# Matrices of shared places by two VectorE comparisons in place of a comparison, a matmul and a copy, with every phase's steps set anew

## The chip, the cores and the metric

The kernel runs on one core of a Trainium2 chip. Its time is the device time of one execution in microseconds; lower is better. Five queues matter: TensorE (PE, whose weight loads the profile shows apart as PEld), VectorE (DVE), ScalarE (ACT), GpSimd (POOL) and the DMA-issuing queue SP. Each engine executes its own instructions in the order in which they stand in the program.

## The reference

32 graphs of 512 nodes with 128 features each go through two layers of a residual graph network with a layernorm after each. The adjacency matrix is sparse, about one entry in sixteen.

```python
adj = adj + eye;  d = adj.sum(2) ** -0.5
x = layernorm(x + (d[:, :, None] * adj * d[:, None, :]) @ (x @ weight) + bias)

m_j = x @ W1[:D];  m_i = x @ W1[D:]
msg = gelu(layernorm(m_j[:, None] + m_i[:, :, None] + b1))     # one vector for each edge
agg = einsum('bijo,bij->bio', msg, adj)
x = layernorm(x + layernorm(concat([x, agg]) @ W2 + b2))
```

The costly part is `msg`: a 128-wide vector, its layernorm and its gelu for every edge.

## The kernel before, in words

**Edges.** A graph's nodes are cut into C = 4 chunks of 128 (P). The kernel works on edges in blocks of 128 by 128 (16 blocks in a graph, numbered n), lists each node's neighbours by half block with max-8 instructions on DVE, and treats the first four of each list (`SLOTS`) as four slots, t = 0 to 3. Edges that did not fit there share two further slots, t = 4 and 5 (`SHARED = 2`): all remaining edges of a block get a running place from 1 to 256, and a place is served by one of 128 rows in one of the two shared slots.

**Units.** A unit (t, q) is one slot of one chunk. A graph has 20 units in this order: (0,0) to (2,3), then (3,0), (3,1), (4,0), (3,2), (4,1), (3,3), (5,0), (5,1). They are numbered 0 to 19 here, so units 14, 16, 18 and 19 are of shared slots. For each unit PE gathers and adds the two nodes' parts into a tile `u` in PSUM, two tiles in turn (`pairs`, L855 to L875); for t < 4 DVE adds the rest and moves it to SBUF (`sums`, L881); ACT applies the gelu, eight instructions for a unit (`messages`, L914); POOL makes the weighted gather matrices (`weights`, L897 and L901); and PE adds up the result (`aggregate`, L928 and L938). The order is written out by hand in one loop over g, the running number of the unit: at an even g the pairs of two units, at an odd g the aggregates of two earlier ones, messages and sums between them.

**Phases.** Everything else that a graph needs is cut into steps (Python generators, one step up to each `yield`): `layer0` (first layer, transposes, the keys), `lists`, `factors`, `more`, `counts`, `spots`, `sending`, `picks`, `parts`, `own_edges`, `finish`. A unit has two half units, so a graph has 40. The table `PLAN` gives for each step of each phase the half unit, relative to the start of the graph's first unit, at which the step's instructions are put into all queues, between the messages of that half unit. Steps with negative numbers run while the graph before is worked on; modulo 40 they show what they share a half unit with. Within one half unit the phases stand in a fixed order: finish, layer0, lists, factors, more, counts, spots, sending, picks, parts, own_edges.

**Around the change.** `counts` numbers the shared edges: `over` and its sums on DVE give a count for each node and block, a matmul with a triangle matrix (`po`, L620) the running sums, and DVE makes `first` and `last` from it (L623, L625): node p of block n owns the places `first < e <= last`. `spots` turns this into `sj`, one row of zeros and ones over 256 places for each node and block. It works on a pair of blocks at a time: `up_to` marks places up to `last` (L647, two DVE instructions); since `first` of a node is `last` of the node before it, a matmul with `step_down` (ones on the diagonal, minus ones beside it) takes the difference of neighbouring rows (`pj`, L660); a DVE copy moves it from PSUM to `sj` (L655). `sending` multiplies the blocks with `sj` (L676: two matmuls for each of 16 blocks) and ACT copies each result to `sent` (L672). `picks` reads `sent` and writes index lists to DRAM, from which the units of t = 4 and 5 gather.

**PSUM.** One pool `ps` of three banks serves in turn, in program order, all phases: the transposes of `layer0`, its `psup` (read by ACT in L334 and L339), its `pconv` (read by DVE in `y`, L364), `po`, `pj` and the `pl` of `sending`. A bank is used again when its reader has finished.

**Patterns.** The constant `places` is kept as 3 by 86 elements with a gap after each 86.

Of the kernel before, what the change touches and what calls it, by code (L numbers as in the profile page):

```python
# [9 lines left out]
BF16 = mybir.dt.bfloat16  # L10
# [3 lines left out]
ALU = mybir.AluOpType  # L14
# [4 lines left out]
P = 128  # L19
# [6 lines left out]
SHARED = 2  # L26
# [3 lines left out]
DEV = 12  # L30

PLAN = {
    "layer0": [-44, -41, -39, -39, -38, -36, -36, -34, -31, -31, -31, -31, -30, -30, -29, -25, -25, -25, -24, -23, -20, -18, -17, -13],
    "lists": [-20, -20, -20, -20, -18, -18, -18, -18, -17, -13, -13, -13, -13, -13, -13, -13, -12, -11, -10, -9, -8],
    "parts": [-18, -13, -13, -9, -9, -9, -8, -7, -7],
    "factors": [-11, -11, -10, -8, -7, -7, -7, -7, -6],
    "more": [-20, -18, -11, -10, -9, -9, -8, -8, -8, -6, -6, -6, -6, -6, -6, -6, -6, -6],
    "counts": [-5, -5, -4, -4, -4],
    "own_edges": [-6, -4, 21, 29],
    "spots": [-3, -2, -2, -1, 0, 2, 3, 4, 5, 8],  # L40
    "sending": [9, 9, 9, 9, 9, 9, 9, 9, 9, 9, 9, 9, 9, 9, 9, 9, 9],
    "picks": [13, 15, 16, 17, 18, 20, 22, 23, 23, 23, 23, 23],
    "finish": [43, 48, 49, 50, 55, 57, 59, 61, 62, 70, 74, 75, 77],
}


# [19 lines left out]
def sparse_path(ctx, tc, x, adj, w0, b0, w1, b1, g1, be1, w2, b2, g2, be2, out, most, flag):  # L66
# [21 lines left out]
    nc = tc.nc  # L88
# [3 lines left out]
    const = ctx.enter_context(tc.tile_pool(name="const", bufs=1))  # L92
# [13 lines left out]
    ident_h = const.tile([P, P], BF16, name="ident_h")  # L106
# [7 lines left out]
        out=stri, in_=stri, compare_op=ALU.is_ge, fill=0.0, base=-1, pattern=[[1, P]], channel_multiplier=-1  # L114
# [8 lines left out]
    place_w = node.tile([P, 3, n_places // 3], F32, tag="t1", name="place_w")  # L123
    nc.gpsimd.iota(
        place_w,
        pattern=[[n_places // 3, 3], [1, n_places // 3]],
        base=1,
        channel_multiplier=0,
# [1 line left out]
    )  # L130
    places = const.tile([P, 3, n_places // 3 + 2], BF16, name="places")[:, :, : n_places // 3]
    nc.vector.tensor_copy(places, place_w)
    step_down = const.tile([P, P], BF16, name="step_down")
    nc.gpsimd.memset(step_down, -1.0)
    nc.gpsimd.affine_select(
        out=step_down, in_=step_down, compare_op=ALU.is_equal, fill=0.0, base=-1, pattern=[[1, P]],
        channel_multiplier=-1,
    )
    nc.vector.tensor_add(step_down, step_down, ident_h)
    place_k = const.tile([P, SHARED], F32, name="place_k")  # L140
    nc.gpsimd.iota(
        place_k, pattern=[[P, SHARED]], base=1, channel_multiplier=1, allow_small_or_imprecise_dtypes=True
# [6 lines left out]
        nth, pattern=[[1, KEPT]], base=0, channel_multiplier=0, allow_small_or_imprecise_dtypes=True  # L149
# [40 lines left out]
    parts = node.tile([P, 3, D], F32, tag="f0", name="be_parts")  # L190
# [8 lines left out]
    for k in range(4):  # L199
# [5 lines left out]
        out=chunk_of, in_=chunk_of, compare_op=ALU.not_equal, fill=1.0, base=0, pattern=[[-1, C], [-C, P // C]],  # L205
        channel_multiplier=1,
# [50 lines left out]
    def bank(key):  # L257
        return ps.tile([P, 512], F32, tag="ps", name=key)
# [376 lines left out]
    def spots(b):  # L635

        st = state[b]
        sj = big.tile([P, C * C, SHARED * P], F32, tag="sj", name=f"sj_{b}")
        st["sj"] = sj
        last = st["last"]  # L640
        n_pairs = C * C // 2
        up_to, pt = {}, {}
        for k in range(n_pairs + 2):
            if k < n_pairs:
                up_to[k] = node.tile([P, 2, n_places], BF16, tag="up_to", name=f"up_to_{b}_{k}", bufs=2)
                for n in range(2):
                    nc.vector.tensor_scalar(  # L647
                        up_to[k][:, n, :].rearrange("p (k e) -> p k e", k=3),
                        places,
                        last[:, 2 * k + n : 2 * k + n + 1],  # L650
                        None,
                        ALU.is_le,
                    )
            if k >= 2:
                nc.vector.tensor_copy(  # L655
                    sj[:, 2 * k - 4 : 2 * k - 2, :], pt.pop(k - 2).rearrange("p (n e) -> p n e", n=2)
                )
            if 1 <= k <= n_pairs:
                pt[k - 1] = bank(f"pj_{b}_{k}")
                nc.tensor.matmul(pt[k - 1], step_down, up_to.pop(k - 1)[:, :, : SHARED * P], start=True, stop=True)  # L660
            yield

    def sending(b):
# [127 lines left out]
    last, more_t = SLOTS - 1, (SLOTS, SLOTS + 1)  # L791
# [171 lines left out]
    for rank, phase in enumerate((finish, layer0, lists, factors, more, counts, spots, sending, picks, parts, own_edges)):  # L963
        for n, at in enumerate(PLAN[phase.__name__]):
            for b in range(B):
                steps_at.setdefault(at + b * n_steps_b, []).append((rank, b, n, phase))
# [288 lines left out]
def kernel(  # L1255
# [33 lines left out]
    with ExitStack() as inner:  # L1289
        sparse_path(inner, tc, *args, most, flag)  # L1290
# [36 lines left out]
```

## Time and profile before

| what | value |
|---|---|
| median of three runs | 3031.48 us (3030.92 to 3032.12) |
| the profiled execution's own time | 3032.46 us |
| its span, first to last instruction | 3030.8 us |
| granted TensorE clock, mean | 0.988 |
| PE, busy share of the span | 94% |
| PEld | 79% |
| DVE | 80% |
| ACT | 84% |
| POOL | 68% |

The profiled execution lies 1.0 us above the median, so its span and the median can be taken for the same number within 0.03%. Matmuls are pipelined and their ends are modelled, so that a busy PE need not be a PE at its rate; the distance from the start of one matmul to that of the next says more. The busy times of neighbouring DVE instructions can overlap in the same way.

### The profile page before, as it was taken

The page shows a single profiled execution, that of the slowest core. Times are in us where ns is not written, and L with a number is a line of the kernel's source. Part 1 is how long each engine was busy: PE and PEld are TensorE (multiplying, and loading weights), DVE is VectorE, ACT ScalarE, POOL GpSimd, SP SyncE. Part 2 cuts the span into 40 slices and gives each one's busy share as a digit, 9 for nine tenths or more (in the row PEclk, how much of TensorE's full clock was granted, in tenths as well). Part 3 has the DMA queues.
Part 4 walks back from the last instruction along what each step waited for, and adds up shares of the span by engine and source line. Part 5 has one row for each costly group of instructions (what it writes and reads, how often), then busy time and mean ns, then how long its engine had stood idle before and what let it go on. Part 6 is the DMA issues. An engine that isn't in the chain of part 4 may idle for free. (4 is left out here: it accounts for less than half of the span.)

```text
span 3030.8 us, 96573 instructions
## 1 busy us (share of the span) xinstructions
PE 2844.0 (94%) x35522; PEld 2379.5 (79%) x35713; DVE 2423.9 (80%) x9803; ACT 2560.8 (84%) x7873; POOL 2065.0 (68%) x2525
## 2 busy tenths in 40 slices
PE   4999999999999999999999999999999999999996
PEld 2788878878778788788788788788787887887875
DVE  6777888777988777988778988778887779887782
ACT  2888888888888888888888888888888888888885
POOL 3576766676776677766667766767666767766765
PEclk7999999999999999999999999999999999999998
DMA  2344443444443444443445433444434444434441
GB/s 58 73 94 99 103 96 78 94 98 99 98 98 77 97 91 106 98 91 82 90 93 112 96 82 81 98 99 101 96 78 96 97 100 98 98 77 97 88 92 45
DMA packets 593025, 276.14 MB, mean 91 GB/s; under 512 B 456112, under 2 KB 576048, under 8 KB 592544
## 3 DMA queue, kind: packets, MB, share of 16 engines
q1 hardware_dynamic: 592320, 269.41, 40.5%
q8 instruction: 284, 4.65, 0.6%
q14 instruction: 197, 1.61, 0.2%
q0 software_dynamic: 224, 0.46, 0.1%
HBM read 155.45 MB, written 13.63 MB: 56 GB/s over the span
## 5 line engine op out<-in xcount | busy, mean ns | idle before, releaser
L914 ACT ACTIVATE m<-m,r 128x128 f32<-128x128 f32 x4096 | 1263.7, 392 | 18.6 <-DVE m L881 18.5
L881 DVE TENSOR_TENSOR m<-u,ac 128x1024 f32<-128x1024 f32 x512 | 609.6, 1211 | 329.8 <-PE u L863 319.2
L897 POOL TENSOR_TENSOR sw<-mt,a_t 128x512 f32<-128x512 bf16 x512 | 616.4, 1224 | 18.0 <-DMA mt<-s 15.1
L928 PE MATMUL agg<-m,sw 128*64 128x128 f32 x8192 | 515.3, 277 | 3.1 <-POOL sw L897 2.8
L928 PEld LDWEIGHTS agg<-m,sw 128*64 128x64 f32 x8192 | 444.6, 137 | 69.9 <-issue 34.2
L855 PEld LDWEIGHTS <-s 64*128 64x128 bf16 x12288 | 364.8, 94 | 140.0 <-issue 98.2
L870 PE MATMUL u<-ac,sj 128*128 128x128 f32 x2048 | 441.4, 297 | 24.4 <-DVE m L881 18.4
L855 PE MATMUL u<-c,s 64*128 64x128 bf16 x12288 | 433.4, 218 | 13.3 <-DVE s L818 13.1
L243 POOL TENSOR_SCALAR ve_l<-mv_l 128x4 f32<-128x4 f32 x96 | 33.7, 351 | 468.3 <-DVE mv_l L240 468.3
L870 PEld LDWEIGHTS u<-ac,sj 128*128 128x128 f32 x2048 | 325.1, 192 | 32.6 <-DVE m L881 25.7
L872 PE MATMUL u<-c,s 128*128 128x128 bf16 x3072 | 339.5, 220 | 0.0
L672 ACT COPY sent<-pl 128x328 f32<-128x328 f32 x512 | 221.2, 432 | 112.8 <-PE pl L676 57.2
L901 POOL TENSOR_TENSOR sw<-mt,sent 128x512 f32<-128x512 bf16 x256 | 291.4, 1163 | 12.2 <-PE agg L938 8.5
L676 PE MATMUL pl<-a_t,sj 128*128 128x164 f32 x2048 | 297.8, 304 | 0.8 <-ACT aggt L766 0.8
L676 PEld LDWEIGHTS pl<-a_t,sj 128*128 128x128 f32 x2048 | 286.4, 190 | 7.7 <-ACT sent L672 6.6
L914 ACT ACTIVATE m<-u,r_s 128x128 f32<-128x128 f32 x1024 | 272.2, 379 | 8.0 <-PE u L875 5.9
L938 PEld LDWEIGHTS agg<-m,sw 128*128 128x128 f32 x2048 | 236.4, 192 | 52.8 <-issue 51.6
L872 PEld LDWEIGHTS <-s 128*128 128x128 bf16 x3072 | 259.9, 99 | 12.1
L938 PE MATMUL agg<-m,sw 128*128 128x128 f32 x2048 | 250.6, 278 | 0.1
L513 DVE FIND_INDEX8 idx<-top,key 128x8 uint32<-128x64 f32 x1024 | 210.1, 218 | 0.0
L581 DVE MATCH_REPLACE8 key<-top,key 128x64 f32<-128x64 f32 x1024 | 205.8, 208 | 0.0
L863 PE MATMUL u<-be_d,sd_rows 64*128 64x512 bf16 x1024 | 195.5, 378 | 0.0
(214 smaller groups left out, 5641.8 us busy)
## 6 DMA issues: line engine op xcount, KB each, us to landing
raw<-idx_d SPq DMA_DIRECT2D x256, 256.5 KB
raw<-idx_ds SPq DMA_DIRECT2D x64, 513.0 KB
a_nat<-in_adj_dram SPq DMA_DIRECT2D x32, 1024.0 KB
sd_rows<-sd_d SPq DMA_DIRECT2D x768, 12.0 KB
xs<-in_x_dram SPq DMA_DIRECT2D x32, 256.0 KB
out_dram<-o_sb SPq DMA_DIRECT2D x32, 256.0 KB
sd_d<-sd_p SPq DMA_DIRECT2D x256, 12.0 KB
mt<-s SPq DMA_TRANSPOSE x192
```

Source lines behind the costliest of these rows:

```text
L513: nc.vector.max_index(idx[:, n - 1, h, :], top[:, n - 1, h, :], half(n - 1, h))
L672: nc.scalar.copy(sent[:, n - 1], pt[:, : SHARED * WIDE].rearrange("p (k w) -> p k w", w=WIDE))
L676: nc.tensor.matmul(pt[:, k * WIDE : (k + 1) * WIDE], sj[:, n, k * P : (k + 1) * P], at[:, n, :], start=True, stop=True,)
L855: nc.tensor.matmul(pu[:, h, c, :], s[halved(h), c, q * P : (q + 1) * P], c3[halved(h), k, c, :], start=(c == 0 and k == 0), stop=False,)
L870: nc.tensor.matmul(pu[:, h, c, :], place, st["ac"][:, q_h, 0, :], start=(c == 0), stop=False)
L872: nc.tensor.matmul(pu[:, h, c, :], s[:, c, q_h * P : (q_h + 1) * P], c3[:, k, c, :], start=False, stop=False)
L881: nc.vector.tensor_tensor(u.rearrange("p h c d -> p (h c) d"), pu.rearrange("p h c d -> p (h c) d"), bcast(state[b]["ac"][:, q, 0, :], 2 * C),
L897: nc.gpsimd.tensor_tensor(sw, mt[:, :, q, :], st["a_t"][:, q, :, :P], ALU.mult)
L901: nc.gpsimd.tensor_tensor(sw, mt[:, :, q_h, :], a, ALU.mult)
L914: nc.scalar.activation(m[:, h, c, :], u[:, h, c, :], AF.Gelu, scale=r[:, k : k + 1])
L928: nc.tensor.matmul(agg[halved(h), c, :], sw[0][:, c, halved(h)], m[:, h, c, :], start=(begin and c == 0), stop=(end and c == C - 1),)
L938: nc.tensor.matmul(agg[:, c, :], sw[h][:, c, :], m[:, h, c, :], start=False, stop=(end and h == 1 and c == C - 1),)
```

## The change

`step_down` goes, with its two POOL instructions and its DVE addition at the start of the program. A constant `places_1` comes, the places 1 to 256 in one row without gaps, in bf16. In `spots` the matmul and the copy from PSUM go; for each block one DVE instruction compares `places_1` with `first` (greater than) and multiplies by `up_to`, and writes `sj`. `spots` has nine steps now, not ten. All eleven rows of `PLAN` have new numbers; the loop over the units is the same.

```diff
 PLAN = {
-    "layer0": [-44, -41, -39, -39, -38, -36, -36, -34, -31, -31, -31, -31, -30, -30, -29, -25, -25, -25, -24, -23, -20, -18, -17, -13],
-    "lists": [-20, -20, -20, -20, -18, -18, -18, -18, -17, -13, -13, -13, -13, -13, -13, -13, -12, -11, -10, -9, -8],
-    "parts": [-18, -13, -13, -9, -9, -9, -8, -7, -7],
-    "factors": [-11, -11, -10, -8, -7, -7, -7, -7, -6],
-    "more": [-20, -18, -11, -10, -9, -9, -8, -8, -8, -6, -6, -6, -6, -6, -6, -6, -6, -6],
-    "counts": [-5, -5, -4, -4, -4],
-    "own_edges": [-6, -4, 21, 29],
-    "spots": [-3, -2, -2, -1, 0, 2, 3, 4, 5, 8],
-    "sending": [9, 9, 9, 9, 9, 9, 9, 9, 9, 9, 9, 9, 9, 9, 9, 9, 9],
-    "picks": [13, 15, 16, 17, 18, 20, 22, 23, 23, 23, 23, 23],
-    "finish": [43, 48, 49, 50, 55, 57, 59, 61, 62, 70, 74, 75, 77],
+    "layer0": [-44, -42, -41, -41, -40, -40, -39, -38, -36, -35, -35, -33, -33, -33, -33, -32, -31, -31, -30, -29, -28, -25, -23, -20],
+    "lists": [-28, -26, -25, -24, -24, -24, -24, -24, -22, -19, -17, -17, -17, -17, -17, -17, -14, -13, -11, -11, -8],
+    "parts": [-20, -17, -16, -14, -10, -10, -6, -6, -5],
+    "factors": [-15, -15, -14, -11, -10, -9, -8, -8, -6],
+    "more": [-15, -12, -12, -9, -9, -8, -8, -8, -8, -7, -5, -5, -5, -5, -5, -5, -5, -5],
+    "counts": [-4, -3, -1, -1, -1],
+    "own_edges": [13, 19, 25, 27],
+    "spots": [-1, -1, -1, 1, 1, 1, 1, 1, 3],
+    "sending": [0, 2, 2, 2, 2, 2, 2, 2, 2, 2, 2, 4, 5, 5, 5, 5, 8],
+    "picks": [10, 11, 11, 12, 13, 14, 15, 16, 16, 16, 17, 18],
+    "finish": [42, 44, 45, 46, 46, 51, 52, 54, 59, 68, 73, 73, 75],
 }
...
-    step_down = const.tile([P, P], BF16, name="step_down")
-    nc.gpsimd.memset(step_down, -1.0)
-    nc.gpsimd.affine_select(
...
-    nc.vector.tensor_add(step_down, step_down, ident_h)
+    places_1 = const.tile([P, SHARED * P], BF16, name="places_1")
+    nc.vector.tensor_copy(places_1, place_w.rearrange("p k e -> p (k e)")[:, : SHARED * P])
...
-            if k >= 2:
-                nc.vector.tensor_copy(
-                    sj[:, 2 * k - 4 : 2 * k - 2, :], pt.pop(k - 2).rearrange("p (n e) -> p n e", n=2)
-                )
-            if 1 <= k <= n_pairs:
-                pt[k - 1] = bank(f"pj_{b}_{k}")
-                nc.tensor.matmul(pt[k - 1], step_down, up_to.pop(k - 1)[:, :, : SHARED * P], start=True, stop=True)
+            if k:
+                before = up_to.pop(k - 1)
+                for n in range(2):
+                    at_n = 2 * k - 2 + n
+                    nc.vector.scalar_tensor_tensor(
+                        sj[:, at_n, :], places_1, first[:, at_n : at_n + 1], before[:, n, : SHARED * P],
+                        ALU.is_gt, ALU.mult,
+                    )
```

More of the change, by code (lines that the diff above doesn't have):

```diff
@@ L132, in sparse_path @@
     nc.vector.tensor_copy(places, place_w)
-    step_down = const.tile([P, P], BF16, name="step_down")
-    nc.gpsimd.memset(step_down, -1.0)
-    nc.gpsimd.affine_select(
-        out=step_down, in_=step_down, compare_op=ALU.is_equal, fill=0.0, base=-1, pattern=[[1, P]],
-        channel_multiplier=-1,
-    )
-    nc.vector.tensor_add(step_down, step_down, ident_h)
+    places_1 = const.tile([P, SHARED * P], BF16, name="places_1")
+    nc.vector.tensor_copy(places_1, place_w.rearrange("p k e -> p (k e)")[:, : SHARED * P])
     place_k = const.tile([P, SHARED], F32, name="place_k")
@@ L639, in spots @@
         st["sj"] = sj
-        last = st["last"]
+        first, last = st["first"], st["last"]
         n_pairs = C * C // 2
-        up_to, pt = {}, {}
-        for k in range(n_pairs + 2):
+        up_to = {}
+        for k in range(n_pairs + 1):
             if k < n_pairs:
@@ L653, in spots @@
                     )
-            if k >= 2:
-                nc.vector.tensor_copy(
-                    sj[:, 2 * k - 4 : 2 * k - 2, :], pt.pop(k - 2).rearrange("p (n e) -> p n e", n=2)
-                )
-            if 1 <= k <= n_pairs:
-                pt[k - 1] = bank(f"pj_{b}_{k}")
-                nc.tensor.matmul(pt[k - 1], step_down, up_to.pop(k - 1)[:, :, : SHARED * P], start=True, stop=True)
+            if k:
[6 more added lines that the diff above has]
+                    )
             yield
```

## The prediction

> **What bounds the kernel now.** I read the page first, then the waits, then the stretches of one graph, and last the groups by shape.
>
> ```profile
> PE 2844.0 (94%) x35522; PEld 2379.5 (79%) x35713; DVE 2423.9 (80%) x9803; ACT 2560.8 (84%) x7873; POOL 2065.0 (68%) x2525
> ```
>
> No engine is full on the mean. The waits and two stretches of one graph, cut at the sums of units 0 and 6, show why:
>
> ```profile
> DVE m L881 <- PE u L863: 319.2, 35, 11.6
> ...
> PEld L660 <- DVE sj L655: 43.9, 91, 3.6
> ...
> PE pj L660 <- DVE sj L655: 22.3, 32, 1.7
> ```
>
> ```profile
> core 0: us, PE busy (x) PEld busy (x) DVE busy (x) ACT busy (x) POOL busy (x), PEclk, DMA share, GB/s
> 1545.50:1578.40 32.90, 32.40 (x383) 29.17 (x383) 18.50 (x34) 27.68 (x82) 19.98 (x26) 1.00 0.46 100
> 1578.40:1637.10 58.70, 55.67 (x736) 44.77 (x735) 56.87 (x272) 52.25 (x165) 44.33 (x53) 1.00 0.41 91
> ```
>
> A graph is two regimes in turn. For 32.9 us PE sets the pace (busy 32.4) and DVE does 18.5 us of work; at its end DVE waits about 9.9 us for PE, the 319.2 us of the first row. For 58.7 us DVE is full (56.9). Together 91.6 us; the first executions of L623, one a graph, go from 71.6 to 2916.2 us, so a graph takes 2844.6 / 31 = 91.8 us. The rest, some 186 us, is the first graph's start and the last one's end.
>
> **The instructions exchanged.** Groups by shape:
>
> ```profile
> L655 DVE COPY sj<-pj 128x512 f32<-128x512 f32 x256 | 174.0, 680 | 2.2 <-PE pj L660 2.2
> L647 DVE TENSOR_SCALAR up_to<-places,last 128x258 bf16<-128x258 bf16 x512 | 149.2, 338 | 29.5 <-PE pj L660 29.5
> L415 DVE SCALAR_TENSOR_TENSOR key<-pv,a_sum,c_sum 128x512 f32<-128x512 f32 x128 | 94.8, 741 | 19.8 <-issue 14.2 <-ACT m L914 3.0
> L364 DVE SCALAR_TENSOR_TENSOR y<-pconv,dinv,xb 128x128 f32<-128x128 f32 x128 | 36.0, 344 | 94.5 <-PE pconv L357 94.5
> ```
>
> ```profile
> L660 PE MATMUL pj<-up_to,step_down 128*128 128x512 bf16 x256 | 83.9, 387 | 24.7 <-DVE sj L655 22.3 <-DVE up_to L647 1.9
> ```
>
> PE loses 256 matmuls: 83.9 us busy, of which about 256 x 0.216 = 55 us are its own (matmuls of this shape start 0.216 us apart when they follow each other), and 66.2 us of waits for the `sj` copies (43.9 + 22.3). That is at most 3.8 us a graph, 1.7 of it work. DVE loses the copies, 174.0 us, and gains 512 instructions that read two rows of 256 elements. The only row of that form from SBUF, L185, ran once, 345 ns at 128 elements, as from PSUM. Upper end: the line through 344 ns at 128 and 741 ns at 512 elements gives 476 ns at 256. Lower end: `up_to`, the same length with one input, 149.2 / 512 = 291 ns. I take 450 ns, near the form's own line, less some overlap. DVE: 230 - 174 = +56 us (-25 to +70), 1.8 us a graph. So work moves from PE to DVE. In the start, two POOL and one DVE instruction go and one DVE cast of 0.4 us comes, beside loads: nothing; the uncovered cost would be 1 us.
>
> **A cost that the durations don't hold: POOL.** The new instruction reads two SBUF tensors; the copy read only PSUM. Rows of the timeline and of single lines show what DVE and POOL do to each other:
>
> ```profile
> 1399.59 0.69 DVE L707 TENSOR_TENSOR kept<-chosen,sent 128x512 f32<-128x512 bf16 x1
> 1399.75 0.62 POOL L243 TENSOR_SCALAR ve_l<-mv_l 128x4 f32<-128x4 f32 x1 [10.86 <-DVE mv_l L240]
> ```
>
> ```profile
> L243 POOL TENSOR_SCALAR ve_l<-mv_l x96: 215/221/650, 26.8 to 3021.3; 128x4 f32<-128x4 f32 x96
> ```
>
> ```profile
> L343 DVE TENSOR_SCALAR mask<-a_t x32: 1227/1992/2273, 19.1 to 2842.2; 128x2048 bf16<-128x2048 f32 x32
> ```
>
> ```profile
> L897 POOL TENSOR_TENSOR sw<-mt,a_t x512: 1148/1164/2161, 77.7 to 2987.7; 128x512 f32<-128x512 bf16 x171
> ```
>
> L243 takes 221 ns, but 620 to 650 while L707, also with two SBUF inputs, runs: it ends with it. L343 takes 1.23 us at best but 1.99 at the median, when POOL's `xb` is under way at its start, and the L897 after it takes 2.15 instead of 1.16. So one holds the other up: POOL behind a two-input DVE instruction, DVE behind POOL by 0.77 us at the median, though that is shown for another form. L707 itself is never slower than 693 ns, but it only meets POOL's short or narrow operations. Bounds for one new instruction: 0 (as L707) and 0.77 us. I take 0.25: POOL is busy 64.31 of 91.6 us, and half of an L897 (0.58) with a chance of 0.7 is 0.41 for the first of two; the second follows it directly and mostly finds POOL held (0.1).
>
> [...]
>
> **The moved steps.** I laid each step's instructions, at their own lengths (start to next start where they follow closely), on the units in which PLAN puts them. Microseconds a graph, before to after:
>
> | units | PE | DVE |
> |---|---|---|
> | 0 to 5 | 31.4 to 35.7 | 18.4 to 26.1 |
> | 6 to 17 | 39.4 to 33.1 | 52.2 to 44.8 |
> | 18, 19 | 10.5 to 10.7 | 4.9 to 6.9 |
>
> The DVE regime is relieved: `picks` (3.7) goes to units up to 5, `counts` (1.9) to 18 and 19, 1.7 of `finish` and a layernorm go early. About 5.4 us of `layer0`'s matmuls go from PE's slack into PE's regime. `sending` leaves half unit 9, where it ran 9.31 us without a break, for 0 to 8, ten of its steps in half unit 2. ACT's 80.0 and POOL's 64.3 us keep their sums; ACT in 6 to 17 falls from 44.4 to 40.3, POOL stays at 38. DMA: `layer0` still loads at -44, the lists leave at -8 and the factors at -6 as before; the index and factor writes of `picks` go from half units 20 and 23 to 14 and 18, past the reads for unit 12 on SP's queue, and the output from 77 to 75. Waits for these reads are small (4.2 us for `raw` from `picks`, 15.1 us for `mt` in all): a gain of 4 us at most, a loss of 15 if a write that waits for ACT holds SP; I take 0.
>
> **The sum.** Before: DVE's 52.2 + 4.9 = 57.1 fill the 58.7 us up to unit 0's sum (1.6 idle); PE's 31.4 and 0.9 of unit 6's pairs fill 32.9 (0.6 idle): 91.6.
> After, up to unit 0's sum: 44.8 + 6.9 + 1.6 = 53.3. From that sum (time 0) PE isn't free: with three banks `pl` 2 needs the bank of `pl` 0, whose copy stands on ACT behind four messages and the eight `s` and `own_s` of `layer0`: 1.14 (sum) + 4 x 1263.7 / 4096 = 1.23 + (35.6 + 36.6) / 32 = 2.26 + 0.43 = 5.1. Then nine blocks at 0.56 (four starts of 0.139): 10.1; PE's units 2 to 5, 22.6, and 0.9: 33.6. A second wait: `pl` 13 needs the bank of `pconv`, read by `y` on DVE, behind unit 0's sum, five pairs of blocks (7.1), the next sum (1.1), `agg_sb` (0.6), `mask` (1.9), the last pair (0.9), a gather (1.2), unit 2's sum (1.1) and itself (1.0): 16.2, while PE is there at 15.2: 1.0. Sum 53.3 + 34.6 + 0.6 = 88.5, 3.1 below 91.6, if POOL costs nothing.
> With 16 x 0.25 = 4.0 us of POOL's holds: those before unit 0's sum delay it, the others delay `y` and the sum of unit 1, where PE now waits with no slack; all of it counts: 92.5, which is 0.9 above 91.6 (31 x 0.9 = 28 us; start and end of the program I leave as they are, +-5). The profiled execution's span, 3030.8, stands for the median, 3031.5: 3059.
>
> **Rivals.** (1) POOL's operations don't hold the new instruction, or it falls into POOL's pauses: 31 x -3.1 = -96, 2935; with a hold of 0.1 us (1.6 a graph) 2985. It decides below 0.19 us each, where 3.1 is used up. For it: L707's steady 692; against: L343. (2) The two cancel, 3025 to 3037. (3) The holds reach 0.41 for each, 6.6 a graph: 95.1, 3140; at 0.77 it would be 12.3 and 3316, which POOL's work in that stretch hardly has room for. (4) DVE stays the bound of units 6 to 17 in name only: ACT (40.3) and POOL (38) are within 7 us of its 44.8 and bunched (POOL 16.3 in units 6 to 9, DVE 13.3): up to 3 us, +93, on top of (1): back to 3028. That the change doesn't do what it says can be left out: in the built program's order PE has 512 instructions fewer, weights included, and DVE 256 more.
>
> **Chances.** The forecast, slower with holds near 0.25 us (3038 to 3110): 0.44. Rival 1, with (4) or without: 0.36. Rival 2: 0.08. Rival 3: 0.12. What a measurement can tell from no change is 0.2%, 6 us. Faster 0.36, same 0.08, slower 0.56. Range 2935 to 3150, rival 1's floor to just over rival 3's first price; the forecast's own range is 3038 to 3110. An instruction of 291 or 476 ns moves all by -50 or +11.
>
> **What would show it.** New `sj` rows well over 450 ns or with a wide spread, and L897, L901 or L330 beside them at over 1.3 us, show the holds; a steady 450 and a graph near 88 us show rival 1. `pl` waiting for `sent`, and again for `y`, shows the banks. PE's waits for `sj` (66.2 us) should be gone, and the 9.9 us pause of DVE before unit 6 shorter. The forecast fails if the period falls although the holds show, because DVE has slack there that I count as path.

## The result, and the profile after

The changed kernel takes 3120.64 us (median of 4 runs, 3117.89 to 3127.39) against 3031.2 for the kernel before on the same chip: 1.0298 times as long, 95% interval 1.028 to 1.0316. That is 89 us more, 2.8 us a graph. The forecast was 28 us more (3059, with 3038 to 3110 around it). Its direction was right, the size was not, and most of this document is about the missing 61 us. The profiled execution has a span of 3116.2 us.

The page of the changed kernel, busy times, to be set against the first fence of the prediction:

```profile
PE 2859.2 (92%) x35457; PEld 2376.1 (76%) x35457; DVE 2584.9 (83%) x10059; ACT 2562.8 (82%) x7873; POOL 2073.5 (67%) x2523
```

256 products are gone, and PE's busy time has hardly changed. That it reads 15 us higher says little: the trace of before holds 35713 weight loads but only 35522 products. The missing 191 are half of the products of two lines, and dropping half of the same products from the trace of after lowers its busy time by 16 to 22 us. DVE is busy for 161 us more, not the 56 of the durations. The waits of the changed kernel (line waited for, total us, times, longest):

```profile
DVE first L618 <- PE po L615: 193.2, 32, 9.8
...
ACT m L910 <- DVE m L877: 75.9, 57, 6.9
PEld agg L924 <- POOL sw L893: 71.9, 33, 3.4
PE agg L924 <- POOL sw L893: 63.8, 31, 3.2
PEld pa L293 <- DMA a_nat<-in_adj_dram: 60.1, 30, 4.7
...
PE pa L293 <- DMA a_nat<-in_adj_dram: 53.4, 31, 4.3
...
DVE m L877 <- PE u L859: 25.9, 19, 5.1
```

The old first row, DVE waiting for `u` ahead of unit 6 (319.2 us), is down to 25.9, as the prediction said, and PE's rows with `sj` are gone from this list. In their place stand three waits that the kernel before had hardly or not at all. The largest is new: DVE waits 6.0 us a graph for `po`, the running sums of `counts` (0.3 us in all before). The other two are PE's own: 2.0 us a graph for POOL's weights (2.8 us in all before), 1.7 for the adjacency matrix (5.1 in all).

One graph of the changed kernel, cut at the sums of units 0, 6 and the next graph's unit 0, as in the prediction:

```profile
core 0: us, PE busy (x) PEld busy (x) DVE busy (x) ACT busy (x) POOL busy (x), PEclk, DMA share, GB/s
1588.69:1625.80 37.11, 35.28 (x387) 29.83 (x388) 31.69 (x65) 28.72 (x86) 20.32 (x27) 1.00 0.17 36
1625.80:1684.31 58.51, 53.98 (x720) 44.30 (x714) 49.30 (x251) 50.03 (x159) 44.22 (x52) 0.94 0.56 124
```

In the second row DVE is busy for 49.3 of 58.5 us; before it was 56.9 of 58.7. DVE lost 7.6 us of work there and the stretch stayed as long as it was. The column PEclk has 0.94 where before had 1.00 in both rows; that is the second trail. Over the 25 graphs in the middle (read from the starts of L877) the stretches are 37.4 and 57.2 us, the period 94.5; before, 91.8.

The new instruction, line view, minimum, median and maximum in ns, then the group with its mean:

```profile
L653 DVE SCALAR_TENSOR_TENSOR sj<-places,first,up_to x512: 467/476/1499, 79.8 to 3017.7; 128x256 f32<-128x256 bf16 x171
```

```profile
L653 DVE SCALAR_TENSOR_TENSOR sj<-places,first,up_to 128x256 f32<-128x256 bf16 x512 | 329.5, 683 | 0.0
```

It takes 476 ns at the median and 683 on the mean: 0.207 us of holding for each, 3.3 us a graph (forecast: 0.25, 4.0). The timeline shows whom it meets:

```profile
1497.77 0.87 DVE L653 SCALAR_TENSOR_TENSOR sj<-places,first,up_to 128x256 f32<-128x256 bf16 x2
...
1499.12 1.27 POOL L325 TENSOR_TENSOR xb<-xs,b_row 128x512 f32<-128x512 f32 x1
1499.20 2.78 DVE L653 SCALAR_TENSOR_TENSOR sj<-places,first,up_to 128x256 f32<-128x256 bf16 x2
1500.35 2.66 POOL L893 TENSOR_TENSOR sw<-mt,a_t 128x512 f32<-128x512 bf16 x2
```

The first pair takes 0.87 us; the next takes 2.78 while POOL's L325 and then L893 run. In the whole trace 153 of the 512 instructions take more than 0.56 us. Each of them overlaps one of POOL's three operations on two full tensors (L325, L347, L893); of the 359 shorter ones only four touch one of the three.

### The profile page after: what moved, and what is told of

Read it like the earlier page. It is cut to its first block, busy times and chain, and to the rows that moved or that the text cites. A ratio compares the mean times of both kernels' runs of the same rounds, so it can differ in the third digit from the quotient of the medians.

```text
span 3116.2 us, 96952 instructions
## 1 busy us (share of the span) xinstructions
PE 2859.2 (92%) x35457; PEld 2376.1 (76%) x35457; DVE 2584.9 (83%) x10059; ACT 2562.8 (82%) x7873; POOL 2073.5 (67%) x2523
## 5 line engine op out<-in xcount | busy, mean ns | idle before, releaser
L877 DVE TENSOR_TENSOR m<-u,ac 128x1024 f32<-128x1024 f32 x512 | 613.1, 1208 | 26.8 <-PE u L859 25.9
L893 POOL TENSOR_TENSOR sw<-mt,a_t 128x512 f32<-128x512 bf16 x512 | 607.6, 1197 | 16.5 <-DMA mt<-s 16.4
L924 PE MATMUL agg<-m,sw 128*64 128x128 f32 x8192 | 525.4, 279 | 65.5 <-POOL sw L893 63.8
L851 PEld LDWEIGHTS <-s 64*128 64x128 bf16 x12288 | 375.5, 96 | 184.9 <-issue 133.8
L851 PE MATMUL u<-c,s 64*128 64x128 bf16 x12288 | 444.5, 221 | 60.2 <-DVE m L877 46.1
L866 PE MATMUL u<-ac,sj 128*128 128x128 f32 x2048 | 445.2, 299 | 15.2 <-DVE m L877 15.1
L672 PE MATMUL pl<-a_t,sj 128*128 128x164 f32 x2048 | 323.8, 307 | 8.5 <-ACT own_s L334 4.9
L653 DVE SCALAR_TENSOR_TENSOR sj<-places,first,up_to 128x256 f32<-128x256 bf16 x512 | 329.5, 683 | 0.0
L238 POOL TENSOR_SCALAR ve_l<-mv_l 128x4 f32<-128x4 f32 x96 | 21.3, 222 | 380.1 <-DVE mv_l L235 380.1
```

The source lines that it names most:

```text
L653: nc.vector.scalar_tensor_tensor(sj[:, at_n, :], places_1, first[:, at_n : at_n + 1], before[:, n, : SHARED * P], ALU.is_gt, ALU.mult,)
L672: nc.tensor.matmul(pt[:, k * WIDE : (k + 1) * WIDE], sj[:, n, k * P : (k + 1) * P], at[:, n, :], start=True, stop=True,)
L851: nc.tensor.matmul(pu[:, h, c, :], s[halved(h), c, q * P : (q + 1) * P], c3[halved(h), k, c, :], start=(c == 0 and k == 0), stop=False,)
L866: nc.tensor.matmul(pu[:, h, c, :], place, st["ac"][:, q_h, 0, :], start=(c == 0), stop=False)
L877: nc.vector.tensor_tensor(u.rearrange("p h c d -> p (h c) d"), pu.rearrange("p h c d -> p (h c) d"), bcast(state[b]["ac"][:, q, 0, :], 2 * C),
L893: nc.gpsimd.tensor_tensor(sw, mt[:, :, q, :], st["a_t"][:, q, :, :P], ALU.mult)
```

## The experiments

In all tables a pair's cost is the mean of its first and of its second instruction for one block (16 blocks a graph). "Half-rate" is worked out from the granted clock in the trace: half of the time spent at 0.50, in us a graph, over the 25 middle graphs. The runs come from several chips; the kernel before took 3031 to 3034 us on each, and ratios are to those.

### 1. The moved `counts`

```diff
-    "counts": [-4, -3, -1, -1, -1],
+    "counts": [-5, -5, -4, -4, -4],
```

> The changed kernel with one row of PLAN put back: counts at [-5, -5, -4, -4, -4]. Theory A (the wait for po: counts now stands on PE behind the shared units' pairs, two aggregates and layer0's transposes, and DVE, idle for 6.0 us a graph, starts spots late): the wait of first for po falls from 193 us to under 30, and the time by 2 to 4 us a graph, to 3000 to 3060. Theory B (POOL's holds on the new instruction, 16 x 0.21 = 3.3 us a graph, are the loss): the holds stay, the time stays within 1 us a graph, 3090 to 3130.

Measured: 3076.29 us, ratio 1.0139 (1.0123 to 1.0156). That lies between the two theories: half of the loss, some 44 us, was in this row. The timelines of PE and then of DVE in the changed kernel show why:

```profile
1485.29 1.95 PE L934 MATMUL agg<-m,sw 128*128 128x128 f32 x16
1487.16 1.09 PE L924 MATMUL agg<-m,sw 128*64 128x128 f32 x16
1488.19 0.66 PE L259 MATMUL pt_x<-ident,xs 128*128 128x128 f32 x4
1489.90 1.09 PE L293 MATMUL pa<-ident,a_nat 128*128 128x128 f32 x8 [1.06 <-DMA a_nat<-in_adj_dram]
1490.83 0.17 PE L615 MATMUL po<-count_h,stri 128*128 128x16 bf16 x1
```

```profile
1484.89 0.31 DVE L607 CAST count_h<-count 128x16 bf16<-128x16 f32 x1
1491.07 0.17 DVE L618 COPY first<-po 128x16 f32<-128x16 f32 x1 [5.87 <-PE po L615]
```

DVE has the counts ready at 1485.2. The product it needs takes 0.17 us, but in PE's queue it stands behind the aggregates of two units, the transposes of `xs`, a wait for a DMA and the transposes of the next adjacency matrix. With `counts` at -5 and -4 the wait for `po` falls from 6.0 to 0.74 us a graph:

```profile
DVE first L618 <- PE po L615: 23.8, 32, 0.8
```

### 2. The transposes that wait for the DMA

```diff
-    "layer0": [-44, -42, -41, -41, -40, -40, -39, -38, ...
+    "layer0": [-44, -42, -39, -39, -39, -39, -38, -38, ...
```
(on top of experiment 1)

> The changed kernel with counts at -5 and -4 as before and, besides, the transposes of the next adjacency matrix at half units -39 and -38 (five steps of layer0) in place of -41 to -39, so that the load has some four microseconds more. Theory A (PE's wait for that load, 49.1 us in all with the early counts, stands on the path): the wait goes and the period falls by up to 1.5 us: 3030 to 3060. Theory B (the transposes only wait where PE has nothing else that is due, or push something else back by as much): within 10 us of 3076, or above.

Measured: 3090.73, ratio 1.0195 (1.0178 to 1.0212), slower than 3076. PE's wait for the adjacency matrix falls from 49.1 to 5.7 us, but `y` now waits 140.6 us for `pconv` (78.5 without this edit) and PE waits 54.0 us (13.3 without it) for the bank that `own_s` frees. Theory B: the stretch up to unit 0's sum became 1.6 us shorter, and the one behind it, in which PE is full, 2.4 us longer.

### 3. Operations and steps crossed

The old instructions on the new steps, and the new ones on the old steps (`spots` of the new ones: -3, -2, -1, 0, 2, 3, 4, 5, 8).

> The operations of before (comparison, matmul, copy) on the new PLAN, spots at [-1, -1, -1, 1, 1, 1, 1, 1, 1, 3]. Theory A: the wait for po stays, and the time is within 1 us a graph of the changed kernel, 3090 to 3150. Theory B: without the holds it is 3.3 us a graph faster than the changed kernel, about 3018, or up to 1.7 us a graph more than that for the matmuls, 3070.

> The new operations on the PLAN of before, spots at [-3, -2, -1, 0, 2, 3, 4, 5, 8]. Theory A: no wait for po, and near before, within 1 us a graph: 3000 to 3062. Theory B: the sj rows again have a mean near 0.68 us against a median of 0.476, and the time is 3 us a graph over before, 3110 to 3140.

Measured: 3403.91 (1.1221, 1.1199 to 1.1242) and 3096.27 (1.0211, 1.0194 to 1.0228). The first missed both theories: with six steps of `spots` in one half unit the products ask for the three banks one after the other (`up_to` waits 101.2 us for `pj`, `sent` 380.2 for `pl`), and its half-rate time is 4.5 us a graph. It does not price the exchange. The second lies between its two theories; its half-rate time is 0.34 us a graph. On the steps of before the new instructions alone cost 63 us, in the three groups that stand ahead of unit 0's sum: the stretch from unit 17's sum to unit 0's grows from 17.2 to 19.9 us, DVE busy for 19.2 of it.

A second try with `spots` spread two by two (-3, -3, -2, -2, -1, -1, 0, 0, 1 and 1), `counts` early, both kinds of instructions:

> The instructions of before (comparison, product, copy) on the new steps, with counts at half units -5 and -4 as before, and the ten steps of spots spread two by two over half units -3 to 1, so that the banks of the products are not all asked for in one half unit. Theory A (the moved steps are sound apart from counts, and the rest of the loss is the instructions): faster than the new instructions with the early counts (3076) by about the 2.0 us a graph that they cost on the old steps: 3000 to 3030. Theory B (the moved steps themselves cost, through other waits than that for po): 3060 or more.

> The new instructions on the same steps as the run with the instructions of before (counts at -5 and -4, spots two by two over -3 to 1). Theory A: more of DVE's work stands ahead of unit 0's sum than with early counts alone (3076), so 3076 to 3100, and 2 us a graph (62 us) above its partner with the instructions of before. Theory B (the place of DVE's work does not matter, only PE's sum): within 5 us of 3076, and within 20 us of its partner.

Measured: 3161.51 (1.0429, 1.0412 to 1.0446) and 3215.89 (1.0617, 1.0599 to 1.0635). The exchange costs 54 us here, close to the second run's 62 and to the 63 above. But both stand far above 3076, as theory B of the first run said: for the new instructions the other place of `spots` costs 140 us. `pl` waits 107.3 us on PE for the bank that `own_s` frees, a wait of 13.3 in the run with early `counts` alone. (Experiment 6 brings in a second difference: half-rate time is 0.55 us a graph in the first of these runs and 3.28 in the second, so that the 54 us are not the exchange's alone.)

### 4. Is DVE's time free behind unit 0's sum?

```diff
-    "spots": [-3, -2, -1, 0, 2, 3, 4, 5, 8],
+    "spots": [0, 1, 2, 3, 4, 5, 6, 7, 8],
```
(new instructions, other steps of before)

> The new instructions on the steps of before, with the nine steps of spots moved from -3 to 8 to 0 to 8, one in each half unit: all of DVE's new work stands behind unit 0's sum, in the stretch in which DVE waited 9.6 us a graph for PE. Theory A (two regimes; DVE's time costs only up to unit 0's sum, and costs nothing behind it until the 9.6 us are used up): the stretch up to unit 0's sum loses three groups of up to 2.3 us against the run of the new instructions on the old steps (93.76 us a graph) and 2 us against before (91.76), and the other stretch keeps PE's pace: 88 to 90.5 us a graph, 2915 to 2995 us, faster than before. Theory B (PE's order, not DVE, sets the length of the stretch up to unit 0's sum): 3030 to 3090.

Measured: 3154.03 us, ratio 1.041 (1.0393 to 1.0428), a miss of both. The stretch up to unit 0's sum did shrink as theory A said (19.9 to 15.2 us). But units 0 to 4 grew by 6.1 us, and DVE kept its 9.9 us of idle time ahead of unit 6. That pause begins when `sending`, which needs the rows that `spots` makes, already runs; nothing of `spots` can move into it. My "DVE has slack while PE sets the pace" was true of the stretch and not of the place. The half-rate time is 2.66 us a graph here, so this run does not price the place alone.

### 5. A bank in place of the second SBUF input

```diff
-                up_to[k] = node.tile([P, 2, n_places], BF16, tag="up_to", ...)
+                up_to[k] = bank(f"pj_{b}_{k}").rearrange("p (n e) -> p n e", n=2)
```

> The changed kernel, but up_to is written to a PSUM bank, so that the new instruction has one SBUF input, places_1. Its rows should be steady near 0.5 us, without holds, if these come from two SBUF inputs. Theory A: the time falls by under 1 us a graph, 3090 to 3120 (the banks are used as the matmul used them). Theory B: it falls by 3.3 us a graph, to about 3018.

> The new instruction on the steps of before, but the last-place comparison is written into a PSUM bank in float32, so that the new instruction reads only one tensor from SBUF and POOL cannot hold it. Theory A (the holds, about 0.33 us each on this plan: mean 0.805 against a base of 0.476, are part of the loss of 63 us that the instructions alone made on the old steps): the new row becomes steady near 0.47 us, the comparison into PSUM costs 0.48 instead of 0.34, so DVE saves 16 x 0.19 = 3 us a graph, 1.1 of it in the three groups that stand before unit 0's sum: about 3055 us; two banks wait as before (up to +20). Theory B (it is the number of DVE instructions and not the holds): no faster than 3085.

Measured: 3431.4 on the new steps (1.1314, 1.1295 to 1.1332), a miss of both theories, where the banks stall as in experiment 3 (`sent` waits 444.0 us for `pl`), and 3111.02 on the old ones (1.026, 1.0243 to 1.0277). The new row on the old steps:

```profile
L653 DVE SCALAR_TENSOR_TENSOR sj<-places,first,pj x512: 465/473/478, 74.0 to 3011.0; 128x256 f32<-128x256 bf16 x171
```

With one SBUF input in place of two the spread is gone here: 478 ns at most, where the mean on the same steps was 805 in experiment 3. The stretch from unit 17's sum to unit 0's gave back 1.85 of the 2.6 us that it had lost, but the transposes now wait for banks (`pa` for `sj`, 37.8 us on PE), the half-rate time is 1.02 us a graph against 0.34, and the run was slower than 3096. The time is theory B's, the reason is not: the holds did cost there, and something else cost more. Another way without holds and without banks was needed.

### 6. Two instructions with one input each

The place minus `first` minus one is negative in front of the node's places. Its bits, read as an unsigned number, are then larger than those of any count, so one comparison with the count (`length`, the bits of the node's count, one more small DVE instruction a graph) does what two did:

```diff
                     nc.vector.tensor_scalar(
-                        up_to[...], places, last[...], None, ALU.is_le)
+                        up_to[...], places, first[...], 1.0, ALU.subtract, ALU.subtract)
...
-                    nc.vector.scalar_tensor_tensor(
-                        sj[...], places_1, first[...], before[...], ALU.is_gt, ALU.mult)
+                    nc.vector.tensor_scalar(
+                        sj[...], before[...].bitcast(uint16), length[...], None, ALU.is_lt)
```

> Steps of before. The matrices from two instructions with one input each: first the place minus the node's first place minus one, in bf16; then the bits of that, read as an unsigned number (a negative one is larger than any positive one), compared with the bits of the node's count. No product, no copy, no bank, and no instruction with two SBUF inputs. Theory A (what the changed instructions cost is DVE's time for the form with two inputs, 0.805 us each on these steps, in the three groups ahead of unit 0's sum): each of the second instructions takes about 0.34 and holds nothing, DVE saves 7 us a graph against the changed instructions on these steps (3096), 2.7 of it ahead of unit 0's sum, and ends at or below before: 2980 to 3030. Theory B (losing PE's products and copies as such brings nothing, and the loss came from elsewhere): 3070 to 3100.

> The same one-input instructions on the new steps with counts early (partner: 3076 with the two-input form). Theory A: DVE saves 5 to 7 us a graph at half units -1 to 3, behind unit 0's sum, where it was full (9.8 of 9.95, 6.4 of 6.4 us): 1.5 to 4 us of the period, 2950 to 3030. Theory B (there PE and the banks set the pace, not DVE): 3060 to 3080.

> The same one-input instructions on the changed kernel as it is, counts late (partner: 3121). If the wait for the running sums of counts and the cost of the two-input form add up, this run stands above the one with early counts by the same 45 us, +-15, by which the two-input pair stands apart, and below 3121 by as much as that one is below 3076. If the two hide each other, the two differences are smaller than 20.

Measured: 3116.55 us on the old steps (ratio 1.0268, 1.0231 to 1.0305), 3052.59 with `counts` early (1.007, 1.0053 to 1.0087), 3122.82 on the changed steps (1.0303, 1.0286 to 1.0321). The first is above what both theories said, the second between them, and the third stands 70 us above the second, not 45. The durations were not the expected ones either (line view, changed steps):

```profile
L645 DVE TENSOR_SCALAR up_to<-places,first x512: 280/298/1421, 78.4 to 3014.6; 128x258 bf16<-128x258 bf16 x171
```

```profile
L657 DVE TENSOR_SCALAR sj<-up_to,length x512: 456/480/484, 79.4 to 3018.0; 128x258 f32<-128x258 uint16 x171
```

The second has a steady 0.48, not 0.34. The first, with gaps in input and output, is quicker at its best than the 0.338 of before and is held up to 1.42, though it has one input. On the changed steps the pair cost 0.989 against 1.023, so that run says little of the holds; with `counts` early it saved 3.3 us of DVE a graph and 24 us in all.

The old steps are the riddle: fewer holds, no banks, no product, and 20 us slower than with two inputs. The granted clock points to the answer, which experiment 7 tests. Two windows of this run, cut where the clock changes:

```profile
core 0: us, PE busy (x) PEld busy (x) DVE busy (x) ACT busy (x) POOL busy (x), PEclk, DMA share, GB/s
1605.09:1608.50 3.41, 1.45 (x40) 1.15 (x41) 3.38 (x7) 2.87 (x11) 3.25 (x7) 0.99 0.94 191
1608.50:1611.91 3.41, 3.41 (x30) 2.89 (x25) 3.38 (x4) 3.41 (x13) 3.41 (x3) 0.51 0.35 99
```

PE has a pause (it is busy for 1.45 of 3.41 us), and for the next 3.41 us it gets half its clock (PEclk 0.51), just when it is busy throughout. This run has 2.80 us of half-rate time a graph; the kernel before has none in these 25 graphs. The changed kernel has 1.43, and the same picture (PEclk 1.00, then 0.50):

```profile
1638.98:1642.40 3.42, 1.40 (x20) 0.92 (x19) 3.42 (x16) 3.42 (x13) 3.34 (x4) 1.00 0.72 85
1642.40:1645.81 3.41, 3.41 (x20) 2.69 (x20) 3.04 (x29) 2.25 (x8) 2.93 (x5) 0.50 0.81 221
```

### 7. PE's pauses filled

Products of constants, read by nobody, on top of the kernel's own work: eight ahead of the aggregate of unit 9 and six ahead of the transposes on the new steps; one in each step of `spots`, in the place of the old `pj`, on the old ones.

```diff
+    def warm(n, name):
+        pw = bank(f"warm_{name}")
+        for _ in range(n):
+            nc.tensor.matmul(pw, ident_h, be_s, start=True, stop=True)
```

The runs with other instructions use the pair of experiment 6, with the gaps taken out of the output of the first and the input of the second.

> The changed kernel's steps, counts late, with two instructions of one input each whose patterns are those of the comparison of before (gaps in one operand only), which POOL never held there (328 to 352 ns): 0.34 and 0.47 us, the same length as the changed kernel's 0.34 and 0.476 at best, so that the holds alone go. Theory A (the prediction's: all of the holds, 16 x 0.207 = 3.3 us a graph, lengthen the graph): 3120 - 100 = 3020. Theory B (the holds fall where DVE has slack, or where the wait for the running sums stands behind them anyway): 3105 to 3125.

> The changed kernel, with products of constants that nobody reads put into PE's two longest pauses: eight before the aggregate of unit 9, where PE waits 2.02 us a graph for weights from POOL, and six before the transposes that wait 1.66 us for the adjacency matrix. Theory C (a pause makes the clock fall to half for the next 3.41 us in some graphs, after it was never below 1.00 in the graphs of before; by the records half-rate time costs at most 1.43 us a graph, 1.16 of it behind these two pauses): 3120 - 36 = 3085, the mean clock up from 0.974 to 0.985 or more. Theory D (the clock falls where PE has slack): 3115 to 3130, whatever the clock.

> Steps of before, the two one-input instructions without holds, and in each step of spots one product of constants that nobody reads, at the place of the product of before. Theory C (the product that went had kept PE busy enough for the full clock; without it the one-input pair lost 2.8 us a graph to half-rate stretches and took 3117): no half-rate stretches, 3117 - 87 = 3030, and somewhat less as the holds of that run (2.1 us a graph) go too: 3000 to 3035. Theory D: 3085 to 3120.

> All that the runs point to on the new steps: counts early, the two one-input instructions without holds, and PE's two pauses filled. Partner: 3053 (one-input pair with holds on the first instruction, 2.1 us a graph, and 1.43 us of half-rate time). Theory C with holds on the path: 2960 to 3010. Theory C with holds off it: 3005 to 3025. Theory D with holds off it: 3045 to 3060.

| run | `counts` | PE filled | pair, us | half-rate | us | ratio (95%) |
|---|---|---|---|---|---|---|
| changed kernel | late | no | 1.02 | 1.43 | 3120.64 | 1.028 to 1.0316 |
| changed kernel, filled | late | yes | 1.03 | 0.14 | 3113.17 | 1.0257 to 1.0291 |
| shorter pair | late | no | 0.87 | 1.16 | 3082.63 | 1.0157 to 1.019 |
| all three | early | yes | 0.97 | 0.07 | 3050.51 | 1.0035 to 1.0068 |
| old steps, filled | old | yes | 1.02 | 0.14 | 3061.27 | 1.0086 to 1.0119 |

Filling takes most of the half-rate time away everywhere (1.43 to 0.14 on the changed kernel, 2.80 to 0.14 on the old steps). On the changed kernel it returns some 7 us, which is not clear of noise (the intervals overlap); the mean clock goes from 0.974 to 0.989 and the time hardly follows. At 2 us below its range that is theory D: behind these two pauses PE is mostly not what the graph waits for. On the old steps 3116.55 becomes 3061.27 although the pair there is longer (1.02 against 0.94): 55 us, between the two theories, with the sign of theory C. The gain lies where PE sets the pace: from unit 0's sum to unit 6's the stretch falls from 35.7 to 31.6 us, and the rest grows by 1.8. The products also take banks, but a better order of the banks is no rival: unfilled, `pl` waits 6.6 us in all for a bank and `pa` not at all; filled, the products themselves wait 27.0 us for banks. The shorter pair with `counts` late returns 38 us for 2.45 us of DVE a graph, between its two theories. All three together have theory D's number, and are only 2 us below the run with `counts` early of experiment 6, whose pair was shorter (0.92 against 0.97). None of these pairs was quite free of holds. With the gaps gone on both sides the second instruction is held (changed steps):

```profile
L657 DVE TENSOR_SCALAR sj<-up_to,length x512: 335/356/1252, 77.9 to 2971.6; 128x258 f32<-128x258 uint16 x171
```

### 8. All causes taken away, and a kernel that beats both

Gaps in one operand of each instruction only: the first reads without gaps and writes with them, the second the other way round.

> Steps of before, one product of constants in each step of spots, and the two one-input instructions once more with gaps in one operand of each only, first in the output, then in the input: by the runs so far this should make the first 0.34 and the second 0.47 us and steady (in the last run on these steps, 3061, the second had no gaps, 0.34 us at best but 0.683 on the mean, so POOL held it by 0.3). DVE saves 16 x 0.21 = 3.4 us a graph, 1.3 of it ahead of unit 0's sum. Theory A (holds on the path where DVE is full): 2985 to 3030, faster than before. Theory B (PE's order sets the length): 3045 to 3065.

> The new steps with counts early, PE's two pauses filled, and the same steady pair: all three causes taken away from the changed kernel, which leaves its moved steps and an instruction pair of 0.81 us. Partner: 3051, where the second instruction was held (0.634 on the mean). DVE saves 16 x 0.16 = 2.6 us a graph behind unit 0's sum, where it is full. Theory A: the sum of the three causes is all of the 89 us, 3010 to 3040. Theory B (holds no longer on the path once counts is early): 3045 to 3060, and something else is left.

On the old steps:

```profile
L650 DVE TENSOR_SCALAR up_to<-places,first x512: 329/338/348, 72.8 to 2920.4; 128x258 bf16<-128x258 bf16 x171
...
L663 DVE TENSOR_SCALAR sj<-up_to,length x512: 464/479/484, 73.9 to 2923.2; 128x258 f32<-128x258 uint16 x171
```

Steady, 0.82 us for a pair, and no hold. Measured on the old steps: 3019.26 us, ratio 0.995 (0.9937 to 0.9964). It beats both kernels, the one before by 14 us, and is 42 us below its partner with holds (3061). On the changed steps with `counts` early and PE filled: 3036.1, ratio 1.0013 (1.0004 to 1.0022), 84 of the 89 us. Its partner with holds took 3050.51. Both have theory A's number. So taking away the late `counts`, the holds and the half-rate time returns 84 us together. That is not quite the same as their share of the loss, since the steady pair on the old steps is quicker than the kernel before. The rest of the moved steps brings nothing: with the same pair and its pauses filled the new order is 17 us behind the old one.

## Why the prediction was right or wrong

**What held.** DVE took over work from PE and became longer by more than the durations say; POOL holds the new instruction; the waits for `sj` and the pause ahead of unit 6 went. The instruction itself took 476 ns, the upper end that I gave, not 450 (0.4 us a graph). The hold was 0.207, not 0.25, and that the two are so near is in part luck: I had 0.41 for the first of two instructions and 0.1 for the second, because POOL would then be held. Measured, 87 of 256 first ones are held by 0.50 us and 66 of 256 second ones by 0.96, a mean of 0.17 and 0.25.

**The step that failed: "After, up to unit 0's sum: 44.8 + 6.9 + 1.6 = 53.3".** The stretch took 57.2 us. DVE's work in it came to 48.9, less than my 51.7; the 1.6 us of idle time, taken over from before, came to 8.3. Six of these are the wait for `po`. I had moved `counts` as 1.9 us of DVE's work and had not followed its one product into PE's queue, where it now stands behind two aggregates and behind `layer0`, moved from -39 to -41. I had written of the load "`layer0` still loads at -44 … I take 0": that left out the load's reader, which came two half units earlier and now waits 1.7 us a graph. Experiment 1 puts `counts` back and measures 3076, 17 us above the forecast of 3059: without this wait the sum would nearly have stood, in part because two errors offset each other (54.7 us up to unit 0's sum against 53.3, 38.2 behind it against 39.2).

**"All of it counts" (16 x 0.25 = 4.0 us).** The size was nearly right, the weight was not. Where only the pair changes, DVE's time a graph and the period go together like this: on the changed steps 2.45 us saved give 38 us (1.2 a graph), with `counts` early 3.3 give 24 (0.8), with the pauses filled as well 2.5 give 14 (0.5), on the filled old steps 3.3 give 42 (1.35). A fifth to a half counts, not all: of the 3.3 us of holds that would be some 0.6 to 1.7 us a graph, an estimate, since no run takes the holds alone from the changed kernel.

**The stretch behind unit 0's sum** took 37.4 us; my terms gave 35.2 and the holds, 39.2. `pl` 2 did start 5.15 us after unit 0's sum (5.1 in the sum), and the ninth block from there ended at 10.3 (10.1), but not for my reason: up to `pl` 2 PE is idle for 0.08 us, it has other work, and waits for the bank of `own_s` were 18.9 us in all. The wait of 1.0 for `y` did not come. What followed took 27.1 us, where I had 25.1 and 4.0 of holds. PE was busy for 35.8 of the 37.4 us, so holds on DVE could not all lengthen this stretch. This hid part of the other error: +3.9 and -1.8 us a graph make some +2.0, times 31 the missing 61 us.

**What the prediction did not have at all** is the clock. PE's lost products and waits were counted as PE's gain (at most 3.8 us a graph). PE's busy time hardly changed: 1.43 us a graph of half-rate time, 44 in 31 graphs, came in. On the changed kernel this cost some 7 us, not clear of noise; on the old steps, without the products, 55.

**The rivals.** Rival 1 (no holds: 2935) is refuted in its condition, since the holds came, and in its number: on the changed steps with no holds, early `counts` and a filled PE the time is still 3036. Rival 3's number (3140) is the nearest to 3121, by luck: its holds of 0.41 us did not come. Rival 4 expected DVE to wait for ACT and POOL in units 6 to 17. But for the wait for `po`, DVE's idle time up to unit 0's sum is 2.0 us a graph, against 1.8 before. What did come up is PE's wait of 2.0 us for POOL's weights ahead of the aggregate of unit 9; no run shows what that alone costs.

**Small sums.** The terms ahead of `y` add up to 16.0, not 16.2, and an instruction of 291 or 476 ns would move the time by -79 or +13 us if all 16 count, not by -50 or +11. Neither changes the account.

What stays open: how the three causes overlap on the changed kernel. They were taken away one after the other, and the order decides what each seems worth (`counts` 44 us first; the pair 38 us with `counts` late, 24 with it early). Which of the other moved steps cost the 17 us is open too.

## What to carry to other kernels

When a step is moved, follow each of its instructions into its own queue: a product of 0.17 us that came behind 6 us of others' work cost more than the whole exchange of instructions was forecast to. Work taken from a nearly full TensorE need not be a gain: look for pauses that it filled (on the old steps half-rate time was 2.80 us a graph without the products and 0.14 with others in their place), and read the granted clock by window, not the mean. DVE's slack counts only where the work can be put; a pause behind the consumer is no slack.

## What the runs showed of the hardware that was not expected

**The clock fell after pauses that were far from an idle stretch.** In the trace of the changed kernel, the 25 middle graphs cut on the 3.413 us grid on which the clock changes make 692 windows, 671 of them at full clock. All 20 falls follow windows with PE busy for 0.37 to 1.63 us, 11 to 48% of the window, and no busier window at full clock is followed by one. (A few windows of 1.58 to 1.63 us are not followed by one either, and near the start of the kernel before, at 121.3 us, a fall stands behind a busy window, of 3.3 us.) In the 25 middle graphs of the kernel before the lowest window has 2.0, and there is no fall. The grid stands still while the graph's period of 94.5 us does not fit it, so the same pause is hit in some graphs only: the 2.02 us wait for POOL's weights comes in each of these 25 graphs and brings a fall in 11.

**One input does not make an instruction steady.** The same subtraction took 280/298/1421 ns with gaps of the same pattern on both sides (experiment 6, changed steps), and 329/338/348 with gaps on one side (experiment 8, old steps). The comparison into float32 took 335/356/1252 with none (experiment 7, changed steps) and 464/479/484 with gaps in its input (experiment 8, old steps). In these four rows the quicker form is the one that is held, and the one with gaps on one side alone is slower and steady, as `up_to` of the kernel before is, with gaps in `places` alone (328/338/352). Why the gaps decide it is not shown. That POOL is what holds the two quick forms is my reading from the two-input instruction, whose 153 long executions all overlap POOL's.
